# A four-layer graph network: layer 1's products in float32r pairs, layer 2's heads one at a time

## The chip, the cores and the metric

The kernel runs on one core of a Trainium2 chip. The time is device microseconds (us) of one execution on that core. The kernel before took 6625.57 us, the median of three runs (6622.46 to 6628.0).

## The reference

4096 nodes with 256 features `x`, and one 4096 x 4096 adjacency `adj`, go through four layers. Each adds its output to its input and normalises the rows: `x = layernorm(x + layer(x))`. Every layer is an attention over the neighbours that `adj` allows. The two that the change touches are

```python
# layer 1: one head
H = X @ W_fc + b_fc
scores = (H @ w_att[:d])[:, None] + (H @ w_att[d:])[None, :] + b_att
scores = jnp.where(A > 0, scores, -1e9)
return jax.nn.softmax(scores, axis=1) @ H
# layer 2: 4 heads of 64 features, per head
e = jax.nn.leaky_relu(s_row[:, :, None] + s_col[:, None, :], negative_slope=0.2)
att = jax.nn.softmax(jnp.where(adj > 0, e, -9e15), axis=-1)
out = concatenation over heads of att @ h
y = jax.nn.elu(out) + (x @ Wr + br)
return gamma * layernorm(y) + beta
```

In layer 1 the term of the row drops out of the softmax, because no non-linear function stands between the sum and the softmax. A weight is then exp(s_dst[j]) times a 0/1 mask. In layer 2 the leaky_relu keeps the two terms together, and the weight of a pair is worked out as a maximum of two products. Layer 0 has 8 heads and a bias from the differences of 6 further features of every pair of nodes. Layer 3 runs three one-head attentions with leaky_relu (slope 0.01) and elu, one after another, before it is added to the input.

## The kernel before

**Tiles.** P = 128 partitions. The 4096 source nodes of an attention are NT = 32 tiles `T` of 128. The 4096 target nodes are NIC = 8 chunks `ic` of IC = 512, and a chunk is ITS = 4 tiles `it` of 128. For every chunk, a loop over `T` multiplies the weights of 128 sources and 512 targets with the values of these sources and adds the products in PSUM.

**Layer 0** (`layer0`, L258 to 493) has a code of its own, and the change doesn't touch it. It also writes what the later layers read from DRAM: `mask_d`, the adjacency as bytes by chunk, and `empty_d`, which is 1 for a target without neighbours. Its products on L432 have 128 weight columns and 128 moving columns.

**`attention`** (L499 to 624) serves layer 1 (called with one head and slope `None`), layer 2 (four heads, D = 64 features each) and the three attentions of layer 3 (one head). It has these stages.

1. `project` (L90 to 169) clears a small matrix `amat` (L105), fills it with the score vectors by small DMAs, multiplies it with the weight matrix (`pw`, L112), loads two tiles of nodes at a time, transposes them and multiplies them with the weights. For each `T`, `sink` (L523 to 526) copies the values to `V`, and adds their sum over all nodes to `pcs` on PE.
2. Maxima and shifts of the scores (`spread`, `shifts`), then the exponentials `v`, and `V` times `v` per tile of sources (L548). The last column of `V` starts as 1, so that it holds `v` afterwards and the product with it gives the softmax's denominator.
3. The chunk loop (L555 on). SP loads the chunk's masks (2 MB of bytes for 512 targets, two buffers). Where there is a leaky_relu, SP also loads the rows `R`, on which DVE clamps and ACT exponentiates (L561 to 565).
4. `weights` (L567 to 575): in layer 1 a weight tile is the mask cast to float32 (`nc.any.tensor_copy`, L572), elsewhere one operation on DVE (L574).

For one head, the products (L584) take 128 columns of weights and the 257 columns of `V` and add them into `acc[it]`, two PSUM buffers each. At the chunk's end four small products (L586) give targets without neighbours the mean over all nodes. Then `quotients` (L222 to 230) divides on DVE.

For four heads, layer 2 handles two chunks at a time (`nk` = 2). Its weight tiles hold 128 x 1024 values for both chunks, with 8 buffers. The heads' values are now the weight operand of PE and the weight tile moves past it. Two heads with 64 features each stand side by side in the columns of the array (L602), and the four denominators stand in columns 0, 32, 64 and 96 (L606). The end of a pair copies the sums out of PSUM (L610), transposes them (L615), adds the mean for targets without neighbours (`emp`, `fixed`, L619 to 622) and divides.

**Ends of chunks.** `finish` is `residual_norm` (L232 to 245) for layers 1 and 3, and `finish2` (L655 to 669) for layer 2. `finish2` runs elu (`elu`, L214 to 220), adds the residual, normalises (`moments` L201 to 204 with the batch statistics on L203 and 204; `inv_std` L207 and 208, a square root on ACT and a reciprocal on DVE; `normed` L212), multiplies by gamma and adds beta on POOL, and calls `residual_norm`, which adds the layer's input on POOL (L238) and normalises a second time.

**What sets the order.** The kernel is written with tiles from pools. A scheduler puts each engine's instructions in one fixed order when the kernel is built, and every engine works through its own list in that order. A tile's next use waits for a free buffer of its name. `nc.any` lets the build choose an engine. SP's queue issues the loads of masks, `R`, residuals and nodes and the stores of results; POOL's issues those of weights and score vectors.

Of the kernel before, what the change touches and what calls it, by code (L numbers as in the profile page):

```python
# [36 lines left out]

F32 = mybir.dt.float32
BF16 = mybir.dt.bfloat16
U8 = mybir.dt.uint8
I32 = mybir.dt.int32
AF = mybir.ActivationFunctionType
ALU = mybir.AluOpType
# [4 lines left out]
P = 128  # L51
IC = 512
# [6 lines left out]
def gnn_stack(ctx: ExitStack, tc: tile.TileContext, a: dict, out: bass.AP):  # L59
    nc = tc.nc  # L60
    N = out.shape[0]
    NT = N // P
    NIC = N // IC
    ITS = IC // P
# [434 lines left out]
    def attention(src, w, wt, nh, scores, nf, slope, finish, name, bias=None, pre=None, extra=None):  # L499
# [4 lines left out]
        D = C // nh  # L504
        s = None if slope is None else 1.0 - slope
        with ExitStack() as st:
# [4 lines left out]
            cs = lp.tile([1 if nh == 1 else P, nh, D + 1], F32, name="cs")  # L511
# [42 lines left out]
            nk = 1 if nh == 1 else 2  # L554
            for ic in range(NIC // nk):  # L555
                i0 = ic * nk * IC
                mask = two.tile([P, nk, NT, IC], U8, name="mask")
                for k in range(nk):
                    nc.sync.dma_start(mask[:, k], mask_d[ic * nk + k])
                if s is not None:  # L560
                    R = two.tile([P, nh, nk, IC], F32, name="R")  # L561
                    for h in range(nh):
                        nc.sync.dma_start(R[:, h], f_d[h, i0:i0 + nk * IC].partition_broadcast(P))
                        nc.vector.tensor_scalar(R[:, h], R[:, h], neg_M[:, h:h + 1], neg_m[:, h:h + 1],
                                                ALU.max, ALU.min)
                        nc.scalar.activation(R[:, h], R[:, h], AF.Exp, bias=sc[:, h:h + 1], scale=s)

                def weights(T, h):
                    w = work.tile([P, nk, IC], F32, name="w", bufs=4 * nk)
                    m = mask[:, :, T, :]  # L570
                    if s is None:
                        nc.any.tensor_copy(w, m)  # L572
                    else:
                        nc.vector.scalar_tensor_tensor(w, R[:, h], t_[:, T, h:h + 1], m, ALU.max, ALU.mult)  # L574
                    return w

                if nh == 1:
                    empty = two.tile([1, IC], F32, name="empty")
                    nc.sync.dma_start(empty, empty_d[:, i0:i0 + IC])
                    acc = [ps.tile([P, 1, D + 1], F32, name=f"acc{it}", bufs=2) for it in range(ITS)]  # L580
                    for T in range(NT):
                        w = weights(T, 0)
                        for it in range(ITS):
                            nc.tensor.matmul(acc[it], w[:, 0, it * P:(it + 1) * P], V[:, T], start=T == 0, stop=False)  # L584
                    for it in range(ITS):
                        nc.tensor.matmul(acc[it], empty[:, it * P:(it + 1) * P], cs, start=False, stop=True)  # L586
                    finish(i0, [quotients(sums, nh, it) for it, sums in enumerate(acc)])
                else:


                    if ic == 0:
                        num = [[ps.tile([P, IC], F32, name=f"num{q}{k}") for k in range(nk)] for q in range(nh // 2)]
                        den = [ps.tile([P, IC], F32, name=f"den{k}") for k in range(nk)]
                        for k in range(nk):
                            nc.vector.memset(den[k], 0.0)
                    for T in range(NT):
                        ws = [weights(T, h) for h in range(nh)]
                        edge = dict(start=T == 0, stop=T == NT - 1)
                        for q in range(nh // 2):
                            for k in range(nk):  # L600
                                for e in range(2):
                                    nc.tensor.matmul(num[q][k][e * D:(e + 1) * D, :], V[:, T, 2 * q + e, 0:D],  # L602
                                                     ws[2 * q + e][:, k], **edge)
                        for k in range(nk):
                            for h in range(nh):
                                nc.tensor.matmul(den[k][32 * h:32 * h + 1, :], V[:, T, h, D:], ws[h][:, k], **edge)  # L606
                    for k in range(nk):
                        sb = work.tile([P, nh // 2 + 1, IC], F32, name="sb", bufs=2)
                        for q, t in enumerate([num[0][k], num[1][k], den[k]]):
                            nc.any.tensor_copy(sb[:, q], t)  # L610
                        ys = []
                        for it in range(ITS):
                            pt = ps.tile([P, nh // 2 + 1, P], F32, name="pt", bufs=2)
                            for q in range(nh // 2 + 1):
                                nc.tensor.transpose(pt[:, q], sb[:, q, it * P:(it + 1) * P], ident)  # L615
                            pn = pt[:, 0:nh // 2].rearrange("p q (e d) -> p (q e) d", d=D)
                            pd = pt[:, nh // 2].rearrange("p (h o) -> p h o", h=nh)[:, :, 0:1]
                            emp = work.tile([P, 1], F32, name="emp")
                            nc.vector.tensor_scalar(emp, pd[:, 0], 0.0, None, ALU.is_equal)  # L619
                            fixed = work.tile([P, nh, D + 1], F32, name="fixed")  # L620
                            nc.vector.scalar_tensor_tensor(fixed[:, :, 0:D], cs[:, :, 0:D], emp, pn, ALU.mult, ALU.add)
                            nc.vector.scalar_tensor_tensor(fixed[:, :, D:], cs[:, :, D:], emp, pd, ALU.mult, ALU.add)
                            ys.append(quotients(fixed, nh, it))
                        finish(i0 + k * IC, ys)

    def vector_scores(pairs):

# [124 lines left out]
```

## Time and profile before

The profiled execution took 6622.46 us, 6620.7 us of it the span from the first instruction to the last. Its stages, in us of the span, with the busy time of the three engines that matter:

| stage | from | to | length | PE | DVE | ACT |
|---|---|---|---|---|---|---|
| layer 0 with its start | 0 | 3261 | 3261 | 2956.8 | 2876.8 | 1242.4 |
| layer 1, projection and values | 3261 | 3414 | 153 | 117.5 | 40.0 | 32.0 |
| layer 1, chunks | 3414 | 3876 | 462 | 462.0 | 39.8 | 159.2 |
| layer 2, projection and values | 3876 | 4021 | 145 | 103.7 | 64.4 | 23.1 |
| layer 2, chunks | 4021 | 4840 | 819 | 795.8 | 726.5 | 57.8 |
| layer 3, first projection | 4840 | 5006 | 166 | 119.9 | 62.9 | 40.6 |
| layer 3, first chunks | 5006 | 5467 | 461 | 461.0 | 226.3 | 16.0 |
| rest of layer 3 | 5467 | 6620 | 1153 | 1091.2 | 562.9 | 97.4 |

The page of the profile lists groups of instructions. A line names the source line, the engine, the operation, the output and inputs by the program's names, the shape, and the number of instructions; after the bar come the busy time of the group, the mean duration of one in ns, and the idle time of the engine just before them with what ended most of it. PE is the matmul, PEld the load of its weights, which runs beside it, DVE the vector engine, ACT the scalar engine, POOL the third elementwise engine, and SP the queue of DMA issues. The duration of one matmul is not the distance between two in a stream, since matmuls overlap. That distance is read from a run of many on the chain or the timeline. Stages differ in what limits them, so busy time is read stage by stage.

### The profile page before, as it was taken

The numbers are of one execution on the slowest core, as the hardware profiler recorded it, in microseconds if no ns is written. First come the engines' busy times: TensorE is split into PE (matmuls) and PEld (weight loads), VectorE is DVE, ScalarE is ACT, GpSimd is POOL, SyncE is SP. The second block draws the span as 40 slices with busy tenths as digits, with TensorE's granted clock in tenths as the row PEclk, the third lists the DMA queues.
The fourth block names the chain that finished last, engine by engine and source line by source line (L and its number), as shares of the span: only waits on it lengthen the run. The fifth ranks groups of instructions, "written<-read, shape, count | busy, mean of one in ns | idle before, by whom it ended". The sixth has DMA issues, their size and how long they took to land.

```text
span 6620.7 us, 91628 instructions
## 1 busy us (share of the span) xinstructions
PE 6107.8 (92%) x35562; PEld 4264.3 (64%) x35562; DVE 4599.4 (69%) x10044; ACT 1668.4 (25%) x2199; POOL 520.9 (8%) x769
## 2 busy tenths in 40 slices
PE   3699898999999999999899998999989998999999
PEld 2477676767777676767658872222237885886787
DVE  1599797989999999999710128889844443553555
ACT  2244343433333333333323320000020001001000
POOL 2111111110000000000000000110110000000000
PEclk9799998999999999999989999999989999999999
DMA  7866566653433444333211122110011101111110
GB/s 220 228 155 165 138 161 141 155 110 53 78 67 67 74 70 77 63 65 52 38 61 47 56 63 85 58 51 9 18 50 64 50 24 61 53 53 35 71 63 32
DMA packets 320976, 527.06 MB, mean 80 GB/s; under 512 B 38815, under 2 KB 214959, under 8 KB 315311
## 3 DMA queue, kind: packets, MB, share of 16 engines
q1 hardware_dynamic: 289262, 433.20, 27.8%
q0 software_dynamic: 31280, 88.00, 4.2%
q8 instruction: 281, 4.60, 0.3%
q14 instruction: 153, 1.25, 0.1%
HBM read 403.22 MB, written 117.83 MB: 79 GB/s over the span
## 4 chain that ended last, share of the span: by engine, by line
PE 43%; issue 35%; DVE 13%; POOL 5%; DMA 3%; ACT 1%; POOLq 0%; SPq 0%; ACTq 0%; DVEq 0%
PE acc L584 25%; PE num L602 6%; DVE e L441 5%; DVE d L421 5%; PE den L606 3%; PE ph L160 3%; POOL not_edge_d L279 2%; POOL mask_d L287 1%; PE pcs L526 1%; PE pf L153 1%; PE acc L586 1%; DVE w L574 1%; PE s L432 1%; POOL y L238 1%; PE pt L138 1%
## 5 line engine op out<-in xcount | busy, mean ns | idle before, releaser
L432 PEld LDWEIGHTS s<-kw,d 113*128 113x128 f32 x16384 | 1891.1, 195 | 367.0 <-issue 280.4
L432 PE MATMUL s<-kw,d 113*128 113x128 f32 x16384 | 1942.7, 280 | 155.2 <-DVE emp L481 57.7
L584 PE MATMUL acc<-V,w 128*128 128x257 f32 x8192 | 1794.4, 382 | 49.8 <-DVE w L574 40.3
L584 PEld LDWEIGHTS acc<-V,w 128*128 128x128 f32 x8192 | 1558.3, 191 | 282.7 <-issue 42.8
L434 ACT ACTIVATE e<-s 128x1024 f32<-128x1024 f32 x1024 | 1045.7, 1023 | 1562.2 <-PE s L432 1437.2
L441 DVE SCALAR_TENSOR_TENSOR e<-R,t,e 128x512 f32<-128x512 f32 x2048 | 1376.4, 736 | 57.9 <-ACT e L434 57.8
L421 DVE TENSOR_SCALAR d<-cj,ci 97x256 f32<-97x256 f32 x4096 | 1356.8, 399 | 19.5 <-PE s L432 11.5
L445 PE MATMUL acc<-e,b 128*33 128x512 f32 x4096 | 950.6, 599 | 14.8 <-DVE e L441 14.8
L574 DVE SCALAR_TENSOR_TENSOR w<-R,t__26278,mask 128x1024 f32<-128x1024 f32 x512 | 628.6, 1284 | 56.7 <-PE den L606 54.9
L445 PEld LDWEIGHTS acc<-e,b 128*33 128x33 f32 x4096 | 222.9, 111 | 531.2 <-issue 369.3
L602 PE MATMUL num<-w,V 128*64 128x512 f32 x2048 | 514.8, 607 | 47.4 <-DVE w L574 47.3
L602 PEld LDWEIGHTS num<-w,V 128*64 128x64 f32 x2048 | 146.4, 138 | 405.0 <-issue 264.4
L218 ACT ACTIVATE elu_neg<-elu_neg 128x256 f32<-128x256 f32 x128 | 49.8, 413 | 1253.0 <-DVE elu_neg L217 1253.0
L574 DVE SCALAR_TENSOR_TENSOR w<-R,t__34203,mask 128x512 f32<-128x512 f32 x256 | 192.0, 751 | 229.8 <-PE acc L584 228.7
L574 DVE SCALAR_TENSOR_TENSOR w<-R,t__31506,mask 128x512 f32<-128x512 f32 x256 | 192.0, 751 | 229.1 <-PE acc L584 228.1
L574 DVE SCALAR_TENSOR_TENSOR w<-R,t__36753,mask 128x512 f32<-128x512 f32 x256 | 193.3, 759 | 199.7 <-PE acc L584 198.8
L226 DVE RECIPROCAL rden<-acc 128x1 f32<-128x1 f32 x128 | 20.3, 158 | 425.5 <-PE acc L586 425.5
L287 POOL DMA_DIRECT2D mask_d<-mb x256 | 180.0, 706 | 1686.7 <-DVE mb L286 1600.6
L606 PE MATMUL den<-w,V 128*1 128x512 f32 x2048 | 291.4, 592 | 0.0
L278 ACT ACTIVATE ne<-ai 128x512 f32<-128x512 int32 x256 | 159.3, 627 | 333.7 <-DMA not_edge_d<-ne 259.3
L572 ACT CAST w<-mask 128x512 f32<-128x512 uint8 x254 | 156.6, 618 | 299.4 <-PE acc L584 291.5
L279 POOL DMA_DIRECT2D not_edge_d<-ne x256 | 149.8, 586 | 918.6 <-ACT ne L278 879.0
(185 smaller groups left out, 2447.8 us busy)
## 6 DMA issues: line engine op xcount, KB each, us to landing
mask<-mask_d SPq DMA_DIRECT2D x40, 2048.0 KB
ai<-in_adj SPq DMA_DIRECT2D x256, 256.0 KB
not_edge_d<-ne POOLq DMA_DIRECT2D x256, 256.0 KB, 5.3
at<-in_adjT SPq DMA_DIRECT2D x256, 256.0 KB
d<-not_edge_d SPq DMA_DIRECT2D x128, 512.0 KB
b<-V_d SPq DMA_DIRECT2D x256, 132.0 KB
mask_d<-mb POOLq DMA_DIRECT2D x256, 64.0 KB, 7.2
R<-r_d SPq DMA_DIRECT2D x8, 2048.0 KB
```

What stands on the lines that cost most here:

```text
L160: nc.tensor.matmul(ph, xT[:, kt, t, :], wx[:, kt, :], start=kt == 0, stop=kt == 1 and bias is None)
L279: nc.gpsimd.dma_start(not_edge_d[r0:r0 + P, c0:c0 + CW], ne)
L287: nc.gpsimd.dma_start(mask_d[c0 // IC:(c0 + CW) // IC, :, k // (N // CW), :].rearrange("c p i -> p c i"), mb.rearrange("p (c i) -> p c i", ...
L421: nc.vector.tensor_scalar(d[0:KD, g, :], cj[:, j0:j0 + JR * P], ci[:, 0, k:k + 1], ci[:, 1, k:k + 1], ALU.max, ALU.subtract)
L432: nc.tensor.matmul(s[:, g], d[:, q * 8 + g, (T % JR) * P:(T % JR + 1) * P], kw_flat, start=True, stop=True)
L434: nc.scalar.activation(by_group[:, q * 8:(q + 1) * 8], s, AF.Exp)
L441: nc.vector.scalar_tensor_tensor(e[:, h, :], R[:, h, :], t_[:, T, h:h + 1], e[:, h, :], ALU.max, ALU.mult)
L445: nc.tensor.matmul(acc[h // 2][o:o + D0 + 1, :], b[:, h, :], e[:, h, :], start=T == 0, stop=T == NT - 1)
L574: nc.vector.scalar_tensor_tensor(w, R[:, h], t_[:, T, h:h + 1], m, ALU.max, ALU.mult)
L584: nc.tensor.matmul(acc[it], w[:, 0, it * P:(it + 1) * P], V[:, T], start=T == 0, stop=False)
L602: nc.tensor.matmul(num[q][k][e * D:(e + 1) * D, :], V[:, T, 2 * q + e, 0:D], ws[2 * q + e][:, k], **edge)
L606: nc.tensor.matmul(den[k][32 * h:32 * h + 1, :], V[:, T, h, D:], ws[h][:, k], **edge)
```

## The change

It has two parts.

**Layer 1.** After `V` times `v`, each tile of values is split in two and written to `Vp`, of type float32r. ACT copies the values to the first half[...]. DVE subtracts this from the values and writes the rest to the second half. POOL fills a 258th column with ones, which nobody reads. The 0/1 weights are cast to float32r, and in place of one float32 product of 257 columns per tile there are two float32r products of 258 columns, which add up in the same PSUM tile. These tiles become two floats wider than the 256 features, and the products of layer 3 and of `empty` use their first 257 columns.

**Layer 2.** It works on one chunk at a time again, and one head at a time. The weight tiles are 128 x 512 with 4 buffers, `R` and the masks are loaded per chunk. One product per head takes 65 columns (64 features and the denominator) as PE's weights and moves the 512 columns of the weight tile past them, into `acc[h]`, one PSUM buffer each. Four products with `empty` close the chunk, each followed by a copy out of PSUM and four transposes into `sums[it]`. `emp`, `fixed`, the clearing of `den` and the pairs go away. The sum over all nodes in `sink` uses one column of ones for every layer, where layer 2 used 128.

```diff
-                pcs = pps.tile([1 if nh == 1 else P, nh, D], F32, name="pcs")
+                pcs = pps.tile([1, nh, D], F32, name="pcs")
...
-                    nc.tensor.matmul(pcs, ones[:, 0:1] if nh == 1 else ones, V[:, T, :, 0:D], start=T == 0, stop=T == NT - 1)
+                    nc.tensor.matmul(pcs, ones[:, 0:1], V[:, T, :, 0:D], start=T == 0, stop=T == NT - 1)
...
+            if s is None:
+                Vp = lp.tile([P, NT, 2, D + 2], F32R, name="Vp")
             for T in range(NT):
                 for h in range(nh):
                     nc.vector.tensor_scalar_mul(V[:, T, h, :], V[:, T, h, :], v[:, T, h:h + 1])
+                if s is None:
+                    nc.scalar.copy(Vp[:, T, 0, 0:D + 1], V[:, T, 0, :])
+                    nc.vector.tensor_sub(Vp[:, T, 1, 0:D + 1], V[:, T, 0, :], Vp[:, T, 0, 0:D + 1])
+                    nc.gpsimd.tensor_copy(Vp[:, T, :, D + 1:], ones[:, 0:2].unsqueeze(2))
...
-            nk = 1 if nh == 1 else 2
-            for ic in range(NIC // nk):
-                i0 = ic * nk * IC
-                mask = two.tile([P, nk, NT, IC], U8, name="mask")
-                for k in range(nk):
-                    nc.sync.dma_start(mask[:, k], mask_d[ic * nk + k])
+            for ic in range(NIC):
+                i0 = ic * IC
+                mask = two.tile([P, NT, IC], U8, name="mask")
+                nc.sync.dma_start(mask, mask_d[ic])
+                empty = two.tile([1, IC], F32, name="empty")
+                nc.sync.dma_start(empty, empty_d[:, i0:i0 + IC])
...
-                    w = work.tile([P, nk, IC], F32, name="w", bufs=4 * nk)
+                    w = work.tile([P, IC], F32R if s is None else F32, name="w", bufs=4)
...
-                    acc = [ps.tile([P, 1, D + 1], F32, name=f"acc{it}", bufs=2) for it in range(ITS)]
+                    acc = [ps.tile([P, 1, D + 2], F32, name=f"acc{it}", bufs=2) for it in range(ITS)]
                     for T in range(NT):
                         w = weights(T, 0)
                         for it in range(ITS):
-                            nc.tensor.matmul(acc[it], w[:, 0, it * P:(it + 1) * P], V[:, T], start=T == 0, stop=False)
+                            wt_ = w[:, it * P:(it + 1) * P]
+                            if s is None:
+                                for k in range(2):
+                                    nc.tensor.matmul(acc[it][:, 0, :], wt_, Vp[:, T, k, :], start=T == 0 and k == 0,
+                                                     stop=False)
+                            else:
+                                nc.tensor.matmul(acc[it][:, :, 0:D + 1], wt_, V[:, T], start=T == 0, stop=False)
...
-                        for q in range(nh // 2):
-                            for k in range(nk):
-                                for e in range(2):
-                                    nc.tensor.matmul(num[q][k][e * D:(e + 1) * D, :], V[:, T, 2 * q + e, 0:D],
-                                                     ws[2 * q + e][:, k], **edge)
-                        for k in range(nk):
-                            for h in range(nh):
-                                nc.tensor.matmul(den[k][32 * h:32 * h + 1, :], V[:, T, h, D:], ws[h][:, k], **edge)
...
+                    acc = [ps.tile([D + 1, IC], F32, name=f"acc{h}") for h in range(nh)]
+                    sums = [ps.tile([P, nh, D + 1], F32, name=f"sums{it}") for it in range(ITS)]
                     for T in range(NT):
+                        for h in range(nh):
+                            nc.tensor.matmul(acc[h], V[:, T, h, :], weights(T, h), start=T == 0, stop=False)
+                    for h in range(nh):
+                        nc.tensor.matmul(acc[h], cs[:, h, :], empty, start=False, stop=True)
+                        sb = work.tile([D + 1, IC], F32, name="sb", bufs=2)
+                        nc.any.tensor_copy(sb, acc[h])
                         for it in range(ITS):
+                            nc.tensor.transpose(sums[it][:, h, :], sb[:, it * P:(it + 1) * P],
+                                                ident[0:D + 1, 0:D + 1])
+                finish(i0, [quotients(sums[it], nh, it) for it in range(ITS)])
```

More of the change, by code (lines that the diff above doesn't have):

```diff
@@ L41 @@
 F32 = mybir.dt.float32
+F32R = mybir.dt.float32r
 BF16 = mybir.dt.bfloat16
@@ L510, in attention @@
             v = lp.tile([P, NT, nh], F32, name="v")
-            cs = lp.tile([1 if nh == 1 else P, nh, D + 1], F32, name="cs")
+            cs = lp.tile([1, nh, D + 1], F32, name="cs")
             nc.vector.memset(cs, float(N))
@@ L552, in attention @@
             ps = st.enter_context(tc.tile_pool(name="att_ps", bufs=1, space=PSUM))
-            nk = 1 if nh == 1 else 2
-            for ic in range(NIC // nk):
-                i0 = ic * nk * IC
-                mask = two.tile([P, nk, NT, IC], U8, name="mask")
-                for k in range(nk):
-                    nc.sync.dma_start(mask[:, k], mask_d[ic * nk + k])
+            for ic in range(NIC):
[4 more added lines that the diff above has]
+                nc.sync.dma_start(empty, empty_d[:, i0:i0 + IC])
                 if s is not None:
-                    R = two.tile([P, nh, nk, IC], F32, name="R")
+                    R = two.tile([P, nh, IC], F32, name="R")
                     for h in range(nh):
-                        nc.sync.dma_start(R[:, h], f_d[h, i0:i0 + nk * IC].partition_broadcast(P))
-                        nc.vector.tensor_scalar(R[:, h], R[:, h], neg_M[:, h:h + 1], neg_m[:, h:h + 1],
+                        nc.sync.dma_start(R[:, h, :], f_d[h, i0:i0 + IC].partition_broadcast(P))
+                        nc.vector.tensor_scalar(R[:, h, :], R[:, h, :], neg_M[:, h:h + 1], neg_m[:, h:h + 1],
                                                 ALU.max, ALU.min)
-                        nc.scalar.activation(R[:, h], R[:, h], AF.Exp, bias=sc[:, h:h + 1], scale=s)
+                        nc.scalar.activation(R[:, h, :], R[:, h, :], AF.Exp, bias=sc[:, h:h + 1], scale=s)
                 def weights(T, h):
-                    w = work.tile([P, nk, IC], F32, name="w", bufs=4 * nk)
-                    m = mask[:, :, T, :]
+                    w = work.tile([P, IC], F32R if s is None else F32, name="w", bufs=4)
+                    m = mask[:, T, :]
                     if s is None:
@@ L573, in weights @@
                     else:
-                        nc.vector.scalar_tensor_tensor(w, R[:, h], t_[:, T, h:h + 1], m, ALU.max, ALU.mult)
+                        nc.vector.scalar_tensor_tensor(w, R[:, h, :], t_[:, T, h:h + 1], m, ALU.max, ALU.mult)
                     return w
                 if nh == 1:
-                    empty = two.tile([1, IC], F32, name="empty")
-                    nc.sync.dma_start(empty, empty_d[:, i0:i0 + IC])
-                    acc = [ps.tile([P, 1, D + 1], F32, name=f"acc{it}", bufs=2) for it in range(ITS)]
+                    acc = [ps.tile([P, 1, D + 2], F32, name=f"acc{it}", bufs=2) for it in range(ITS)]
                     for T in range(NT):
@@ L585, in attention @@
                     for it in range(ITS):
-                        nc.tensor.matmul(acc[it], empty[:, it * P:(it + 1) * P], cs, start=False, stop=True)
-                    finish(i0, [quotients(sums, nh, it) for it, sums in enumerate(acc)])
-                else:
-                    if ic == 0:
-                        num = [[ps.tile([P, IC], F32, name=f"num{q}{k}") for k in range(nk)] for q in range(nh // 2)]
-                        den = [ps.tile([P, IC], F32, name=f"den{k}") for k in range(nk)]
-                        for k in range(nk):
-                            nc.vector.memset(den[k], 0.0)
-                    for T in range(NT):
-                        ws = [weights(T, h) for h in range(nh)]
-                        edge = dict(start=T == 0, stop=T == NT - 1)
-                        for q in range(nh // 2):
-                            for k in range(nk):
-                                for e in range(2):
-                                    nc.tensor.matmul(num[q][k][e * D:(e + 1) * D, :], V[:, T, 2 * q + e, 0:D],
-                                                     ws[2 * q + e][:, k], **edge)
-                        for k in range(nk):
-                            for h in range(nh):
[L606 to L611, printed above, removed]
-                        for it in range(ITS):
[L613 to L624, printed above, removed]
@@ new lines, in attention @@
+                        nc.tensor.matmul(acc[it][:, :, 0:D + 1], empty[:, it * P:(it + 1) * P], cs, start=False, stop=True)
+                    sums = [t[:, :, 0:D + 1] for t in acc]
+                else:
+                    acc = [ps.tile([D + 1, IC], F32, name=f"acc{h}") for h in range(nh)]
+                    sums = [ps.tile([P, nh, D + 1], F32, name=f"sums{it}") for it in range(ITS)]
+                    for T in range(NT):
+                        for h in range(nh):
[4 more added lines that the diff above has]
+                        nc.any.tensor_copy(sb, acc[h])
+                        for it in range(ITS):
+                            nc.tensor.transpose(sums[it][:, h, :], sb[:, it * P:(it + 1) * P],
+                                                ident[0:D + 1, 0:D + 1])
```

## The prediction

> **What bounds the kernel now.** I read the page first, then the busy time of each engine by stage, then the chain of work that ended last, then single steps on the timeline. On the page, TensorE (PE) is busy for 92% of the span, and these are the groups that the change touches:
>
> ```profile
> L584 PE MATMUL acc<-V,w 128*128 128x257 f32 x8192 | 1794.4, 382 | 49.8 <-DVE w L574 40.3
> ...
> L574 DVE SCALAR_TENSOR_TENSOR w<-R,t__26278,mask 128x1024 f32<-128x1024 f32 x512 | 628.6, 1284 | 56.7 <-PE den L606 54.9
> ...
> L602 PE MATMUL num<-w,V 128*64 128x512 f32 x2048 | 514.8, 607 | 47.4 <-DVE w L574 47.3
> ```
>
> L584 serves layers 1 and 3: 4 loops of 8 x 32 x 4 = 1024 matmuls are 4096, and there are 8192 records, so each float32 matmul is two records. By stage (columns: stretch, its length, busy PE, PEld, DVE, ACT, POOL, clock, DMA share, GB/s), layer 1's attention loop and layer 2's are:
>
> ```profile
> 3414.00:3876.00 462.00, 461.98 (x2105) 399.91 (x2106) 39.78 (x150) 159.21 (x261) 19.98 (x28) 0.99 0.13 46
> ...
> 4021.00:4840.00 819.00, 795.81 (x4175) 199.12 (x4176) 726.47 (x904) 57.79 (x86) 68.42 (x79) 0.99 0.10 34
> ```
>
> Layer 1 is pure PE: 462 of 462 us. Layer 2 is PE too, with VectorE (DVE) close behind at 89%. The chain gives the pitch of matmuls in a stream (columns: start, us, work):
>
> ```profile
> 2963.37 7.34 PE s L432 x64
> ...
> 3531.90 55.71 PE acc L584 x256
> 3589.54 55.71 PE acc L584 x256
> ```
>
> A layer-1 chunk is 256 records in 55.71 us, 217.6 ns each, and repeats every 57.64 us. A layer-0 record (128 weight columns, 128 moving columns) takes 7.34/64 = 114.7 ns. One double step of layer 2 (two chunks, one T) on the timeline:
>
> ```profile
> 4101.15 3.65 PE L602 MATMUL num<-w,V 128*64 128x512 f32 x16
> 4101.24 4.87 DVE L574 SCALAR_TENSOR_TENSOR w<-R,t__26278,mask 128x1024 f32<-128x1024 f32 x4 [0.54 <-PE den L606]
> ...
> 4104.74 1.90 PE L606 MATMUL den<-w,V 128*1 128x512 f32 x16
> ...
> 4106.56 3.65 PE L602 MATMUL num<-w,V 128*64 128x512 f32 x16
> ```
>
> It repeats in 5.41 us, 2.705 per chunk and T. 128 such steps are 692.5 us, while the loop runs from 4022.96 to 4838.5, 815.5: 123 us go at chunk boundaries, where DVE does layer 2's epilogue and PE waits:
>
> ```profile
> 4215.10 2.26 DVE L212 TENSOR_SCALAR y<-y,mv,rs 128x256 f32<-128x256 f32 x4
> ...
> 4222.48 0.43 DVE L203 BATCH_NORM_STATS2 bn_st<-y 128x6 f32<-128x256 f32 x1 [3.34 <-POOL y L238]
> ...
> 4225.58 1.93 PE L602 MATMUL num<-w,V 128*64 128x512 f32 x4 [1.74 <-DVE w L574]
> ```
>
> And after layer 2, layer 3's projection starts late:
>
> ```profile
> 4867.62 1.84 PE L112 MATMUL pw<-amat,wt_sb 128*128 128x2 f32 x8 [16.21 <-DVE fixed L622]
> ```
>
> [...]LDWEIGHTS: [...]here 33 columns take 111 ns and 128 take 190-195, 0.83-0.88 ns a column[...]. [...]Here two 64-column records share 0.43 us.
>
> **The change, part by part.**
>
> (a) Layer 1's loop. Each 257-column float32 matmul (2 records, 435 ns) becomes two float32r matmuls of 258 columns. Unknown: their pitch. [...]I take the layer-0 record[...]. A chunk falls from 55.71 to 256 x 0.1155 = 29.57. Eight chunks: -209 us. The 1.92 us between chunks (L586) stay. Cover: the casts (L572, 618 ns on ACT, one per T) fit in 0.92 us of PE per T; a mask of 2 MB lands in 8 us against 31.5 per chunk; sqrt of the epilogue stands on ACT behind nine casts of the next chunk, 7 us in, when its input (6.7 us after the chunk's end) is there. Were a cast not covered, each T would cost at most what it exceeds 0.92.
>
> (b) The split of V. Per T, a copy on ACT (about 0.38, as L524's 0.37), a subtraction on DVE (0.34 pitch, as L228), a tiny POOL copy. DVE: 32 x (0.265 + 0.34) = 19.4 us against 8.5 today, but PE takes a T only every 0.92 us, so it runs ahead. On ACT 12 copies come first, which the mask's landing (3413.35, unchanged) hides; then two casts and four copies alternate, 2.8 us per two T where PE uses 1.85. Over five turns, less the two casts given to DVE, I put +4 (bounds 0 and 8).
>
> (c) Layer 2's steps. Four matmuls with 65 weight columns, 512 moving, nothing in parallel: [...]3.44 us per chunk and T. DVE needs 4 x 0.664 = 2.66 (from 1.284 and 4.87 above, halved in columns), so PE stays the bound. (3.44 - 2.705) x 256 = +188.5.
>
> (d) Layer 2's boundaries, walked in the built order; time 0 is the end of a chunk's last product. PE: four products with `empty` (0.86 each), 16 transposes (0.12), 0.2 for the first copy of a sum: 5.6 us. DVE has five weight tiles of the next chunk done at 7.3 (four buffers), then the whole first half of the epilogue in one block: 16 operations at 0.34, 8 at 0.2, 7 at 0.09, 0.7 of dependent waits = 8.3. The sixth tile is there at 16.3; PE ran dry at 10.4: 5.9 us. Three more tiles, R (0.46) and four normalisations (0.44): next tile at 21.4, PE dry at 19.8: 1.7. Then batch statistics wait for POOL, 6.4 to 7.4 us after the first normalisation (4215.10 to 4222.48 above), with only two tiles made: 5. The other two statistics 0.8, the second normalisation 1. Together 14.4 + 5.6 = 20 us, seven times 140, against 123: +17. The doubt is the POOL wait and what covers it: 16 to 24 each, so -11 to +45.
>
> (e) After layer 2. Before, 29.1 us pass from the loop's end (4838.5) to `pw`, since the epilogues of two chunks stand ahead on DVE. Now `amat` is cleared once the last products end, and its small DMAs and weights bring `pw` some 10 us after the loop: -19 (bounds -25 and -8).
>
> (f) Layer 2's projection. The column sum uses one weight column instead of 128[...]: about 0.23 us x 32 = +7 where PE is the bound. The two memsets (1 us) go and R is half as wide for the first step (about 3): -4. I put +2 for the stage. Masks and `R` move on SP's queue by chunk instead of pair; they land 10 us into a 130 us chunk, so nothing is late. Layer 3's loops keep their instructions; 0.
>
> Sum: -209 + 4 + 188.5 + 17 - 19 + 2 = -16.5. The profiled execution took 6622.46 (span 6620.7), the median is 6625.57; 6622.5 - 16.5 = **6606 us**.
>
> **Rivals.** Each nanosecond of pitch in (a) is 2048 records, 2.05 us.
> - *Two cycles per column* (slower): [...]Pitch 217.6, layer 1 gains nothing: 6606 + 209 = 6815. For it: no float32r is in the trace[...]. It decides from 130 ns on (+13 us), break-even is 123.5.
> - *Loads not hidden*: [...]a load of about 53 ns (transposes: 137 against 190 for the plain load) stands between products: pitch 165, 6606 + 101 = 6707. Layer 0 speaks against it.
> - *Boundaries half as bad*: four buffers and DVE's slack of 0.8 us per T absorb half the stall: -50, 6556. Against it: before, with 10.8 us of tiles in hand, PE still waited.
>
> **Chances.** Likeliest case 0.74, its own range 6585 to 6630 (pitch 111 to 122 and boundary 18 to 22); two cycles 0.12; loads 0.08; easy boundaries 0.06. No change is within 0.2%, 13 us, about what a measurement can tell. Of the 0.74, 0.46 is faster, 0.25 the same, 0.03 slower. So faster 0.52, same 0.25, slower 0.23. The range 6578 to 6708 leaves out the two-cycle case and part of the easy boundaries.
>
> **What would show it.** (a) a layer-1 chunk every 31.5 us, records 115 ns apart; two cycles would show 57. (b) the first chunk 4 us longer. (c) 3.44 us per T in layer 2. (d) gaps of 6, 2, 5, 1, 1 us on PE at every chunk, chunk period 130. (e) `pw` 10 us after layer 2's loop. The net is a small difference of two sums near 205, so a pitch 7% off or a boundary 2 us off moves the verdict.

## The result and the profile after

The changed kernel takes 6647.55 us (median of 4 runs, 6643.32 to 6654.52), the kernel before 6624.01 us (6617.52 to 6628.0, 4 runs). The ratio is 1.0038 with a 95% interval of 1.002 to 1.0055: 0.4% slower, where 0.25% faster was forecast. The time lies inside the stated range and outside the likeliest case's own range of 6585 to 6630. The profiled execution took 6646.21 us, 6644.4 of it the span; the two spans differ by 23.7 us, and stage by stage the difference is this:

| stage | before | after | change | predicted |
|---|---|---|---|---|
| up to layer 1's first product | 3414.0 | 3415.8 | +1.8 | 0 |
| layer 1's chunks, with their last products with `empty` | 463.6 | 274.3 | -189.3 | -205 (a, b) |
| from there to layer 2's first product | 145.3 | 152.5 | +7.2 | +2 (f) |
| layer 2's chunks, to the last product with a weight tile | 815.5 | 1032.7 | +217.2 | +205.5 (c, d) |
| from there to layer 3's first product | 167.5 | 151.6 | -15.9 | -19 (e) |
| rest of layer 3 | 1614.7 | 1617.4 | +2.7 | 0 |
| sum | | | +23.7 | -16.5 |

Every stage for which a change was forecast went the way it was said to, and each came out dearer. Two large sums nearly cancel, so 40 us of small misses turn the sign.

These groups of the page after take the place of those shown of before:

```profile
L607 PE MATMUL acc<-w,V 128*65 128x512 f32 x2048 | 932.0, 617 | 87.1 <-DVE w L583 86.8
...
L594 PE MATMUL acc<-Vp,w 128*128 128x258 f32 x2048 | 259.5, 291 | 9.9 <-ACT w L581 9.9
```

Layer 1's 2048 records (L594, as many as float32 made) have 259.5 us of busy time. Layer 2's products are 2048 records in one group, where two groups stood before. The stages of layer 1's and layer 2's chunks, by the busy time in stretches (columns: stretch, length, busy PE, PEld, DVE, ACT, POOL, clock, DMA share, GB/s), show what had not been thought of:

```profile
3415.50:3693.00 277.50, 274.43 (x2112) 269.06 (x2112) 54.90 (x202) 163.78 (x280) 23.39 (x34) 0.96 0.23 79
...
3842.60:4880.00 1037.40, 974.88 (x2232) 307.14 (x2232) 869.53 (x1401) 85.01 (x127) 68.01 (x84) 0.95 0.09 29
```

The clock is 0.96 and 0.95, where both loops had 0.99 before. Summed over the stretches in which TensorE was granted half its clock, layer 1's loop holds 22.6 us of them (5.2 before) and layer 2's 107.8 us (20.9 before).

**Layer 1.** The chain of waits has the chunks one after another (columns: start, us, work):

```profile
3451.32 32.61 PE acc L594 x256
3485.86 32.61 PE acc L594 x256
3520.39 32.66 PE acc L594 x256
3554.98 31.14 PE acc L594 x256
```

Most chunks stream for 32.6 us, one in four for 31.1; 29.6 were forecast. Three stretches round one chunk's end show what lengthens a stream (columns as above):

```profile
3448.68:3452.09 3.41, 3.41 (x21) 2.74 (x21) 1.73 (x7) 1.07 (x2) 1.32 (x2) 1.00 0.97 413
3452.09:3455.50 3.41, 3.41 (x19) 3.41 (x18) 1.17 (x7) 1.24 (x2) 0.98 (x3) 0.50 0.45 174
3455.50:3483.50 28.00, 28.00 (x233) 28.00 (x233) 3.43 (x11) 18.16 (x29) 0.56 (x1) 1.00 0.16 47
```

PE is busy all through, also in the 3.41 us before the clock halves. But these hold the 1.92 us of one-row products with `empty`, which end the chunk at 3451.25. The clock then stays at 0.50 for 3.41 us and comes back. All 62 half-clock stretches of this trace start on multiples of 3.413 us from each other. Of the seven ends between chunks, five had their 1.92 us inside one such step, and a stretch followed each. Two had them split over two steps (3553.0 to 3554.9, where a step ends at 3554.49, and 3655.1 to 3657.1, step end 3656.89), and none followed. At full clock the pitch is 120.8 ns, where 115.5 was taken.

**Layer 2.** A chunk repeats in 131.7 us (130 forecast). The records of PE round one boundary, from the timeline (in brackets the wait before, and what ended it):

```profile
4225.69 4.21 PE L607 MATMUL acc<-w,V 128*65 128x512 f32 x8
4234.60 8.31 PE L607 MATMUL acc<-w,V 128*65 128x512 f32 x12 [4.70 <-DVE w L583]
4246.78 15.64 PE L607 MATMUL acc<-w,V 128*65 128x512 f32 x32 [3.87 <-DVE w L583]
```

There are two waits, 4.7 and 3.9 us, where five of 14.4 together were forecast. Yet the 12 records between them take 8.31 us, and at 0.43 us each they would take 5.16. So the half clock takes back what the waits fall short of the forecast. Over the loop (us in total, number of waits, the longest):

```profile
PE acc L607 <- DVE w L583: 86.8, 20, 24.6
```

Without the 24.6 us ahead of the first chunk, PE waits 62.2 us at seven boundaries, 8.9 each. A chunk's period is 256 x 0.43 = 110.1, plus 5.6 of PE's own work as step (d) has it, plus 8.9, which leaves 7.1 us per boundary to the half clock.

Layer 3's projection is there sooner, as forecast:

```profile
4888.10 1.84 PE L116 MATMUL pw<-amat,wt_sb 128*128 128x2 f32 x8 [2.62 <-DMA amat<-in_L_a]
```

That is 12.7 us after layer 2's last weight product; before it was 29.1, and about 10 were predicted.

### The profile page after: what moved, and what is told of

Read it like the earlier page. It is cut to its first block, busy times and chain, and to the rows that moved or that the text cites. A ratio compares the mean times of both kernels' runs of the same rounds, so it can differ in the third digit from the quotient of the medians.

```text
span 6644.4 us, 87906 instructions
## 1 busy us (share of the span) xinstructions
PE 6102.7 (92%) x33610; PEld 4225.6 (64%) x33610; DVE 4734.5 (71%) x10505; ACT 1701.5 (26%) x2268; POOL 516.5 (8%) x801
## 4 chain that ended last, share of the span: by engine, by line
PE 47%; issue 35%; DVE 10%; POOL 4%; DMA 3%; ACT 1%; POOLq 0%; SPq 0%; ACTq 0%; DVEq 0%
PE acc L597 19%; PE acc L607 13%; DVE e L445 4%; DVE d L425 4%; PE acc L594 3%; PE s L436 3%; PE ph L164 3%; POOL not_edge_d L283 2%; POOL mask_d L291 1%; PE pcs L530 1%; PE acc L449 1%; PE pf L157 1%; PE acc L599 1%; DMA not_edge_d<-ne 1%; PE pt L142 1%
## 5 line engine op out<-in xcount | busy, mean ns | idle before, releaser
L597 PE MATMUL acc<-V,w 128*128 128x257 f32 x6144 | 1347.7, 382 | 40.0 <-DVE w L583 40.0
L597 PEld LDWEIGHTS acc<-V,w 128*128 128x128 f32 x6144 | 1169.3, 191 | 215.9 <-issue 39.6
L607 PE MATMUL acc<-w,V 128*65 128x512 f32 x2048 | 932.0, 617 | 87.1 <-DVE w L583 86.8
L583 DVE SCALAR_TENSOR_TENSOR w<-R,t__27399,mask 128x512 f32<-128x512 f32 x1024 | 771.0, 761 | 134.5 <-PE acc L607 47.9
L607 PEld LDWEIGHTS acc<-w,V 128*65 128x65 f32 x2048 | 288.9, 143 | 713.3 <-DVE w L583 351.6
L583 DVE SCALAR_TENSOR_TENSOR w<-R,t__35356,mask 128x512 f32<-128x512 f32 x256 | 192.0, 751 | 230.2 <-PE acc L597 229.1
L583 DVE SCALAR_TENSOR_TENSOR w<-R,t__32659,mask 128x512 f32<-128x512 f32 x256 | 192.0, 751 | 229.9 <-PE acc L597 228.8
L583 DVE SCALAR_TENSOR_TENSOR w<-R,t__37906,mask 128x512 f32<-128x512 f32 x256 | 193.2, 758 | 200.7 <-PE acc L597 199.8
L594 PE MATMUL acc<-Vp,w 128*128 128x258 f32 x2048 | 259.5, 291 | 9.9 <-ACT w L581 9.9
L594 PEld LDWEIGHTS acc<-Vp,w 128*128 128x128 f32 x2048 | 257.8, 197 | 12.3 <-issue 12.3
L611 ACT COPY sb<-acc 65x512 f32<-65x512 f32 x32 | 18.6, 582 | 748.9 <-PE acc L609 748.9
```

Source lines behind the costliest of these rows:

```text
L583: nc.vector.scalar_tensor_tensor(w, R[:, h, :], t_[:, T, h:h + 1], m, ALU.max, ALU.mult)
L594: nc.tensor.matmul(acc[it][:, 0, :], wt_, Vp[:, T, k, :], start=T == 0 and k == 0, stop=False)
L597: nc.tensor.matmul(acc[it][:, :, 0:D + 1], wt_, V[:, T], start=T == 0, stop=False)
L607: nc.tensor.matmul(acc[h], V[:, T, h, :], weights(T, h), start=T == 0, stop=False)
```

## The experiments

The theory going in: layer 1 gains what float32r saves, less a half-clock stretch that thin work at each chunk's end sets off; layer 2 loses its pairs, and more at its boundaries, where PE's waits set off half-clock stretches too. The rivals: the two parts disturb each other; the stretches come from float32r itself; the pitch is the stream's and not the load's; the boundary's length is VectorE's total of work. The kernels ran on other chips than the first comparison (the kernel before took 6606 to 6610 us there), so ratios and traces are compared.

**Layer 1's part alone.** The kernel before with the first part of the change, and nothing of the second:

```diff
+                Vp = lp.tile([P, NT, 2, D + 2], F32R, name="Vp")
...
-                            nc.tensor.matmul(acc[it], w[:, 0, it * P:(it + 1) * P], V[:, T], start=T == 0, stop=False)
...
+                                for k in range(2):
+                                    nc.tensor.matmul(acc[it][:, 0, :], wt_, Vp[:, T, k, :], start=T == 0 and k == 0,
+                                                     stop=False)
```

> The kernel before with layer 1's part of the change alone; layer 2 keeps its pairs of heads and chunks. Parts add up: layer 1's loop takes 274 us as in the changed kernel, layer 2's loop 815 us as before, and the time is 6624 - 182 = 6442 us, ratio 0.9725. Rival, the parts disturb each other (the half-clock stretches in the changed kernel's layer 2 follow from the denser layer 1): layer 2's loop is longer than 825 us here and holds well over 21 us of half clock.

Measured: 6412.29 us against 6607.77, ratio 0.9706 (0.9691 to 0.972). The two loops of layer 1 and layer 2, by stretches (columns as above):

```profile
3395.00:3667.50 272.50, 271.99 (x2112) 266.41 (x2112) 53.22 (x194) 163.27 (x279) 21.10 (x30) 0.97 0.22 79
3813.00:4629.00 816.00, 794.38 (x4160) 197.78 (x4164) 724.49 (x897) 55.32 (x83) 68.59 (x79) 0.99 0.09 32
```

The parts add up. Layer 2's loop is as before, with 21.0 us of half clock, so the changed kernel's half clock in layer 2 is layer 2's own. The first part gains 2.9% (195 us). Of the 13 us that this is more than the 182 expected, 5.6 are layer 2's projection, which takes 146.8 us here and 152.5 in the changed kernel; the rest is not assigned. By the difference of the two ratios the second part costs 3.3%, about 219 us, where its steps, (c) to (f), were predicted at +188.5 together.

**The thin products spread out.**

```diff
-                                                     stop=False)
+                                                     stop=T == NT - 1 and k == 1)
...
+                        if s is None and T % 8 == 4:
+                            it = T // 8
+                            nc.tensor.matmul(acc[it][:, :, 0:D + 1], empty[:, it * P:(it + 1) * P], cs, start=False, stop=False)
-                    for it in range(ITS):
+                    for it in range(ITS if s is not None else 0):
```

> As the run with layer 1's part alone, but the four one-row products with empty stand behind tiles 4, 12, 20 and 28 of the chunk instead of all at its end. Same products. Theory 1, the 1.92 us of one-row products in one piece brings the half-clock stretch of 3.41 us at the start of the next chunk: these stretches go, chunks take 30.9 us of stream plus 1.9, the loop 274 falls to about 265, the time by about 9 us. Theory 2, the stretch comes from something else at a chunk's start (the mask's load, the float32r stream itself): it stays, the loop is within 2 us of 274.

Measured: ratio 0.9721 (0.9706 to 0.9735), no better than 0.9706. The mechanism held and the gain didn't come. After the start of the first chunk there is no half clock in the loop, though a mask is still loaded at each chunk's start. Yet the loop takes 276.6 us where 265 was expected. The chain has a group of 64 float32r records every 8.54 us:

```profile
3416.24 7.92 PE acc L594 x64
3424.78 7.93 PE acc L594 x64
```

64 records are 7.72 us, so one float32 product with `empty` among float32r products costs 0.82 us in place of 0.48. Four of them cost a chunk 1.4 us more, about what its stretch had cost.

**Fewer columns.** Layer 1's stream is cut for all tiles but the first of a chunk, to 130, 256 and 192 columns (c0 = 128, 2 and 66); the weight loads stay. Theory 1 below lays the pitch to the load, theory 2 to the stream.

```diff
+                                    c0 = 0 if T == 0 else 128
-                                    nc.tensor.matmul(acc[it][:, 0, :], wt_, Vp[:, T, k, :], start=T == 0 and k == 0,
+                                    nc.tensor.matmul(acc[it][:, 0, c0:], wt_, Vp[:, T, k, c0:], start=T == 0 and k == 0,
```

> The changed kernel, with layer 1's products cut to 130 of 258 columns for all tiles but the first of a chunk; it leaves out half of the features' sums. Same weight loads, half the stream. Theory 1, the load of 128 weight columns sets the pitch of 120.7 ns: the pitch stays at 115 to 121 ns. Theory 2, [...]the pitch falls to 60 to 70 ns, and the casts of 618 ns per 8 products (77 ns each) become the limit, a chunk of about 20 us.

The time was 6785.71 us (one execution), 178 more than the kernel before on that chip, with half of layer 1's stream left out. Two stretches inside the loop, products alone (columns: stretch, length, busy PE and PEld, clock, DMA share, GB/s):

```profile
3400.00:3440.00 40.00, 40.00 (x189) 40.00 (x189) 0.50 0.00 1
3576.00:3600.00 24.00, 24.00 (x218) 24.00 (x217) 1.00 0.09 28
```

Nearly the whole loop runs at half clock (399 of 437 us), with 213.6 ns between records, which neither theory had. Only one chunk got the full clock, and there the pitch was 111.7 ns. Taking away half of the stream saves 9 ns of 120.8: the load theory is near, with 111.7 a little under its 115. The full clock ended 9 us into the next chunk, behind a wait. The page has 11.2 us of idle time for these products, of which 9.3 lie ahead of the loop, and the chain shows where the other 1.9 are:

```profile
L595 PE MATMUL acc<-Vp,w 128*128 128x130 f32 (+1 forms) x2048 | 409.0, 395 | 11.2 <-DVE V L554 9.3
```
```profile
3571.51 30.54 PE acc L595 x256
3611.45 43.44 PE acc L595 x208
```

Before the last 208 records of that chunk PE waits for a cast that stands on ACT behind the epilogue's square root. The clock fell at 3612.79 and stayed at half to the end of the loop, with PE never idle.

> The changed kernel, layer 1's products cut to 256 of 258 columns for all tiles but the first of a chunk; it leaves out the sums of two features. At full clock 258 columns had 120.8 ns between records and 130 columns 111.7 ns. If the pitch grows with the stream's length, two columns are worth 0.1 to 0.8 ns: 120 ns or more. If there is a step above 256 columns[...]: 112 to 116 ns, a chunk of 29.7 us or less without a half-clock stretch.

> The changed kernel, layer 1's products cut to 192 columns in the same way; it leaves out a quarter of the features' sums. If the load alone sets a floor of 111.7 ns[...]: 111 to 113 ns at full clock. If load and stream disturb each other in proportion: 116 ns. If thin streams bring the half clock, as with 130 columns[...]: [...]only the stretches at chunk starts stay.

At full clock the mean pitch was 119.1 ns with 256 columns and 111.9 ns with 192. So up to 192 columns there is a floor of 112 ns, which the stream's length doesn't move. What stays the same there is the load of 128 weight columns; its size was not varied. Somewhere between 192 and 256 columns the stream begins to add to the floor, 7 ns by 256. The 119.1 lies between what was expected with a step above 256 columns and without one, and nearer to no step.

With 256 columns half-clock stretches stand at five of the seven chunk starts and nowhere else in the loop after its start. With 192 columns there are six, and only three of them at chunk starts. The other three, against the expectation, begin 8.5 to 9.2 us into a chunk, each right behind a wait of 1.7 to 2.1 us for the same late cast as above. So the clock fell inside a stream with 192 columns as with 130, each time behind a wait; with 192 it came back after one step, with 130 it did not. The times were 6618.4 and 6621.43 us against 6610.15, one execution each.

**Eight weight buffers in layer 2.**

```diff
-                    w = work.tile([P, IC], F32R if s is None else F32, name="w", bufs=4)
+                    w = work.tile([P, IC], F32R if s is None else F32, name="w", bufs=4 if nh == 1 else 8)
```

> The changed kernel with 8 weight buffers in layer 2 instead of 4. Theory 1, the boundary is long because PE has only four tiles ahead when VectorE turns to the epilogue: the first wait of a boundary (4.2 us) falls to about 1, the waits (62 us in the loop) at least halve, half clock (108 us) falls with them, and the loop of 1033 us becomes 985 to 1010. Theory 2, the wait for POOL in the second normalisation and VectorE's own total of work per chunk decide: VectorE has no time to run further ahead, the loop stays within 8 us of 1033.

Measured: 6602.13 us against 6607.77, ratio 0.9995 (0.9986 to 1.0003), where the changed kernel has 1.0038. One boundary on PE:

```profile
4203.42 7.88 PE L607 MATMUL acc<-w,V 128*65 128x512 f32 x14
4211.80 4.51 PE L607 MATMUL acc<-w,V 128*65 128x512 f32 x10 [0.49 <-DVE w L583]
4217.89 2.20 PE L607 MATMUL acc<-w,V 128*65 128x512 f32 x4 [1.58 <-DVE w L583]
4224.18 16.28 PE L607 MATMUL acc<-w,V 128*65 128x512 f32 x33 [4.09 <-DVE w L583]
```

The first wait is all but gone, since PE has 14 records ahead instead of 8, and the loop falls to 1005.9 us, as theory 1 said. The waits fell from 62.2 to 45.8 us, not to half as expected: the last, 4.1 us, stays, and one of 1.6 us is new. Half clock fell from 107.8 to 78.1 us.

**No gamma and beta.**

```diff
-                nc.gpsimd.tensor_mul(y, y, gamma)
-                nc.gpsimd.tensor_add(y, y, beta)
```

> The changed kernel without the multiplication by gamma and the addition of beta on POOL in layer 2's epilogue; it leaves these two out. Theory 1, as predicted the second normalisation waits for POOL: the wait of 3.9 to 4.1 us on PE in the middle of a boundary goes, half clock behind it too, and a chunk of 131.7 us becomes 124 to 128, layer 2's loop 1033 becomes 980 to 1010. Theory 2, VectorE's own work in the boundary (8.3 us in one block and four normalisations) leaves PE dry anyway: the wait turns to another place, the chunk stays above 130.

Measured: 6600.16 us against 6606.22 (one execution). On PE:

```profile
4207.28 4.29 PE L607 MATMUL acc<-w,V 128*65 128x512 f32 x8
4216.20 13.98 PE L607 MATMUL acc<-w,V 128*65 128x512 f32 x24 [4.63 <-DVE w L583]
4230.42 19.96 PE L607 MATMUL acc<-w,V 128*65 128x512 f32 x46 [0.23 <-DVE w L583]
```

The second wait is 0.2 us, the first 4.6 as before. A chunk falls to some 126.8 us, the loop to 998.8. So the second wait is VectorE's for POOL, as step (d) had it. The two waits have two causes, and of these two runs each takes away one. Here too half clock falls, to 80.2 us.

**Float32r for the thin products too.** Layer 1's part alone, with `empty` and `cs` in float32r:

```diff
+                        er = two.tile([1, IC], F32R, name="er")
+                        nc.vector.tensor_copy(er, empty)
...
+                        if s is None:
+                            for k in range(2):
+                                nc.tensor.matmul(acc[it][:, 0, :], er[:, it * P:(it + 1) * P], csr[:, k, :], start=False,
+                                                 stop=k == 1)
+                            continue
```

> As the run with layer 1's part alone (6412 us, ratio 0.9706), but layer 1's products with empty are float32r too: cs split in two halves like the values, two products of 258 columns in place of one float32 product of 257. They stay at the chunk's end. If the piece of thin work there brings the half-clock stretch, its length decides: 8 records of 121 ns are 0.97 us in place of 1.92, no change of type comes in between, the stretches go, and a chunk takes 31.9 us in place of 33.8 on the mean: 15 us less, 6397 us, ratio 0.968. If one-row products bring it however short they are, chunks with a stretch stay at 33.4: 6403 us or more. If the change between types costs nothing and one-row products aren't the cause, 8 us less at most.

Measured: 6395.88 us against 6606.22, ratio 0.968 (0.9664 to 0.9697), which is faster than both kernels and as expected. On PE:

```profile
3429.83 30.50 PE L602 MATMUL acc<-Vp,w 128*128 128x258 f32 x251
3460.26 1.22 PE L609 MATMUL acc<-csr,er 1*128 1x258 f32 x8
```

The eight thin records take 1.2 us, and no chunk after the first has a half-clock stretch. The loop's clock is 0.99, and chunks repeat in 32.27 us. One-row products as such don't set off the stretch: 1.2 us of them don't, where 1.92 us in float32 did. Length and type changed together here. That the length counts with the type kept is seen at the chunk ends of the changed kernel, where 1.92 us split over two steps brought none.

**A long thin end in float32.** In the kernel before:

```diff
-                    for it in range(ITS):
-                        nc.tensor.matmul(acc[it], empty[:, it * P:(it + 1) * P], cs, start=False, stop=True)
+                    for k in range(2 if s is None else 1):
+                        for it in range(ITS):
+                            nc.tensor.matmul(acc[it], empty[:, it * P:(it + 1) * P], cs, start=False, stop=s is not None or k == 1)
```

> The kernel before, with layer 1's four products with empty issued twice; it adds the mean over all nodes twice to targets without neighbours. 3.84 us of one-row float32 products end each chunk, in place of 1.92. If thin work in one piece brings a half-clock stretch whatever the type of the products around it, there is now one of 3.41 us at the start of most of layer 1's chunks (chunk 59.55 us plus about 1.5); the kernel before has none there. If it is float32r that brings it, there is none: 59.55 us each.

Measured: 6628.85 us against 6610.15 (one execution). The chain:

```profile
3457.14 57.39 PE acc L584 x256
3518.20 55.71 PE acc L584 x256
3577.57 57.39 PE acc L584 x256
```

The doubled thin work takes 3.66 us by the trace. Five of seven chunk starts now have the stretch, and each such stream is 1.7 us longer. These five had 2.1 to 3.2 us of thin work within one step of 3.413 us, the other two 1.9 and 2.0. So plain float32 shows the same thing, only at a slightly greater length: 1.92 us never set it off in the kernel before, though three of its chunk ends had all of it in one step.

## Why the prediction was wrong

Two terms failed above all. The pitch in step (a) was put at 115.5 ns and measured 120.8. The clock was put at nothing: half clock costs 7.2 us more than before in layer 1 and 7.1 us at each boundary of layer 2. The terms of (f) and (e) follow with 5.2 and 3.1 us. That the time lies within the stated range is luck: the range reaches up to 6708 for the sake of loads that stand between products, at a pitch of 165 ns, and this did not happen. Pitch and boundary both lie within the likeliest case's own bounds (111 to 122 ns, 18 to 22 us), and the time doesn't.

**Step (a), the pitch, failed in its size.** It took layer 0's record of 114.7 ns and put 0.8 more for two columns, by the author's estimate. The floor under that is 112 ns, with 130 and with 192 columns. But the stream of 258 columns isn't hidden under it: together 120.8. That is 5.3 ns x 2048 = 10.9 us. Why layer 0's float32 record of 128 columns stays nearer to the floor than a float32r one of 256 (119.1) is open. The rival of loads not hidden (165 ns) had a loss of this kind, at ten times the size, and the rival of two cycles per column fell: a pitch of 217.6 was nowhere seen at full clock.

**What step (a) left out was the clock.** It kept the 1.92 us between chunks and took all else at full speed, since the loop before ran at 0.99. Eight streams of 30.92 us would be 247.4; they took 257.2, so half clock took 9.8 us. In the loop before it took 2.6, in its first chunk alone (58.3 us against 55.7); the difference is 7.2. That the thin work at the chunks' end sets it off is shown by three runs: spread out, or shortened, the stretches go; lengthened in float32, they come. In the traces of both kernels each stretch of one clock lasts a whole number of 3.413 us steps. In the five at chunk ends of layer 1's loop that half clock followed PE had no gap; 1.92 us of thin work in one were enough.

What counts as too little work in a step was not shown. Counted by the records that start in them, the steps of layer 1's loop are these. In the changed kernel those five hold 8 thin records and 10 to 12 float32r ones, where a step of stream alone holds 28 or 29; one more with 8 and 12, whose last thin record ends 0.2 us behind it, was followed by full clock. In the kernel before, the three with all the thin work of a chunk's end hold the same 8 and 5 or 6 float32 ones, and full clock came next each time. A half-clock step at the start of a stream holds 15 or 16 records of 258 columns in the changed kernel, and full clock came next. With 130 columns it holds 16 records too (213.6 ns each), yet the clock stayed at half for 399 of 437 us; so the number of records alone does not decide it. The one rise there came in a step with a chunk's first tile (from 3571.51), which has all 258 columns. At 111.7 ns the same 130 columns kept the full clock until a wait came. That float32 stands more thin work because its stream keeps PE at work for longer per column (257 columns in 217.6 ns, 258 of float32r in 120.8) is an estimate of the author's; no run was made to test it.

**Step (b)** said +4; no wait of PE after its first product shows, and the loop begins 1.8 us later, in which layer 0's spread is contained. So (a) and (b) together missed by 15.7 us: 10.9 + 7.2 - 4, and 1.6 not assigned.

**Step (c)** held: 0.43 us per record at full clock, PE the bound. **Step (d)** was right in its place and nearly in its sum (21.6 us each against 20), and wrong in its make-up. The waits for the block of the epilogue and for POOL are there, and each was removed by a run of its own. They are 8.9 us, not 14.4. One reason may be that PE works through its tiles at half clock in between and so needs the next later, which no run isolates; the half clock itself takes 7.1. The easy-boundary rival (half of 14.4) came nearer with the waits and had no clock either. With some 9 us over the seven boundaries and a first chunk 2.6 us too long (5.4 us of half clock), (c) and (d) missed by 11.7 us.

**Steps (e) and (f)** had the right signs. (e) gave 15.9 of 19 us: `pw` came 12.7 us after the loop instead of 10. (f) cost 7.2 and not 2 (its own terms, +7 and -4, make +3). The +7 for the one weight column in `sink` may be the whole of it (two tiles of nodes repeat in 6.82 us, from 3760.89 to 3767.71, and before in 6.29, from 3943.14 to 3949.43), and the -4 for `R` and the memsets did not show. In the three kernels with layer 1's part alone the stage takes 146.0 to 148.6 us, in the six with both parts 151.6 to 153.6, so most of it comes with layer 2's part. What in it costs this was not tried.

So the sum failed by 40 us: 15.7 in layer 1, 11.7 in layer 2's loop, 5.2 and 3.1 in the two projections, 4.5 in stages that don't change. Those 4.5 us lie within what one execution differs from the next (6643 to 6655 us here). The prediction's own warning, that 7% of pitch or 2 us of boundary moves the verdict, is what happened: 5% of pitch, 1.6 us of boundary, and the clock.

## What to carry to other kernels

Look at the granted clock of a stage before pricing a faster version of it. When a stream of products changes its type or is cut into shorter pieces, thin work or waits between the pieces that were free of consequences can begin to cost time after each, as here (some 1.5 us in layer 1, where a chunk streams for 32.6 us with a half-clock stretch and for 31.1 without). In this case it paid to make such work shorter, in the stream's own type, and not to spread it. And where a change joins a gain to a loss of the same size, its parts are worth measuring apart: here the first part alone, with the thin products in float32r, is worth 3.2%.

## What was not expected of the hardware

A kernel with half of layer 1's stream taken out was 178 us slower than the kernel before. With 130 columns per weight load PE stayed at half clock for 399 of 437 us, at 213.6 ns per record against 111.7 in its one chunk at full clock, and a wait of 1.9 us stood where it lost that clock. A float32 product among float32r products cost 0.82 us instead of 0.48 among its like. And 128 weight columns loaded for every 258 streamed cost 120.8 ns per product, 9 more than with 130 streamed (111.7).
